# A four-layer image network on one core: three loads change queue, and four durations in the kernel's planning clock change

## The chip, the cores and the metric
The kernel runs on one core of a Trainium2 chip. The metric is the device time of one execution in microseconds (us), where less is better. A core has TensorE (PE, with its weight loads shown as PEld), VectorE (DVE), ScalarE (ACT), GpSimd (POOL) and SyncE (SP). Each executes its own instructions in program order, and they meet at semaphores. ScalarE, SyncE and GpSimd also issue DMAs.

## The reference
Four images of 96 channels and 64 x 64 pixels (L = 4096 positions) go through four residual layers:

```
x = x + scan_layer(groupnorm(x))        # layer 0: a selective scan in four directions
x = x + deformable_conv(groupnorm(x))   # layer 1: 3 x 3 taps at learned positions
t = x as 4096 tokens of 96 channels
t = t + fourier(layernorm(t));  t = t + ffn8(layernorm(t))    # layer 2
t = t + attention(layernorm(t)); t = t + ffn8(layernorm(t))   # layer 3
```

The scan is the large part. For each image b, direction k (4), channel d (192) and state n (16), position after position:

```
h[d,n] = exp(delta[d] * A[d,n]) * h[d,n] + delta[d] * u[d] * B[n]
y[d]   = sum over n of h[d,n] * C[n]
```

B and C depend on the position and on n, delta and u on the position and on d. `ffn8` rounds the inputs and weights of its two products to an 8-bit float format.

## The kernel before, in words
The scan is cut into 4 images x 4 directions x 4 steps of 1024 positions x 3 groups of 64 channels x 8 units: 1536 units, each a tile of 128 partitions (16 states x 8 channels) by 1024 positions. For each unit:

- `fetch` (L874, ScalarE's queue) loads delta into `da`, repeated over the states, five units ahead. Six buffers.
- `decay` (L895, ScalarE) turns `da` into exp(delta A), two units ahead.
- `inflow` (L901, PE) spreads delta u over the states with two products of 96 x 128 by 96 x 512. The three bfloat16 parts of delta u, which together stand for a float32 value, are summed in the product. The result `db` is in one of two PSUM buffers, one unit ahead.
- `recur` (DVE) multiplies `db` by B (L915), then runs the scan instruction (L918) into `hh`.
- `weigh` (POOL) keeps the last column as the next state (L925) and multiplies `hh` by C (L927).
- `total` (PE, L946) sums over the states of two units into `py`; after eight units `settle` (ACT, L957) copies `py` into `yb` and `store` (SyncE, L964) writes it out.

`fetch_step` loads B and C (`bc`, two issues at L881) once for each step of 1024 positions, that is for 24 units. It does so at n mod 24 = 12, twelve units ahead of their first use. `fetch_block` loads the delta u parts (`du0` and `du1`, two issues at L889) once for eight units. It does so at n mod 8 = 2; `inflow` first needs them at n mod 8 = 7. Both have two buffers.

Around the scan there are two streams of side work, written as Python generators that give out a few instructions and then a `cost`. The stream `ends` does, for every image, the preparation of its scan (convolution, projections, `steps`) and later layers 2 and 3 (`Layers23.image`, which starts by loading `t`). The stream `middle` does the close of layer 0 (`behind`) and layer 1 (`Layer1.image`: offsets, then 288 indirect gathers at L1249, their weighting at L1258, transposes at L1272, the product at L1286 and the result `xo`, stored at L1293). Layers 2 and 3 of an image need its layer 1, which needs its whole scan.

The order of all instructions is fixed when the program is built, by a simulated clock (`Clock`). It keeps a planned end for each of PE, DVE, ACT and POOL. After each unit of the scan, its `unit` adds the least unit time PACE to a due time:

```
def now(self):
    return max(self.ends[DVE], self.due) if self.own is None else self.own
def unit(self, scanned):
    self.due += PACE
```

Then the streams may put in steps as long as `has_room` says that no engine a step uses is planned further ahead of now than `AHEAD` (3 us for PE and DVE, 5 for ACT, 7 for POOL), and that DVE's side work in this unit is under 6 us. Each scan stage adds its own planned time: `inflow` 1.1 on PE, `recur` 1.22 and 2.33 on DVE, `weigh` 2.55 on POOL, `total` 1.5 on PE for two units, and 1.3 more for the first two of eight. A `fetch` of `da` adds 0.6 on ACT; the loads of `bc` and `du` add nothing. So a planned duration decides where instructions stand, not how long they take. When the scan is over, the streams go on alone with five PSUM banks for `ends`.

Of the kernel before, what the change touches and what calls it, by code (L numbers as in the profile page):

```python
# [21 lines left out]
DI, NS, R, KG = 192, 16, 6, 4  # L22
D2 = DI - 128
T = 1024
# [7 lines left out]
D8 = 8  # L32
# [149 lines left out]
def cost(pe=0.0, dve=0.0, act=0.0, pool=0.0, **more):  # L182
    return Step((pe, dve, act, pool), **more)


def wait(us=0.0, **more):

    return Step((0.0,) * 4, us, **more)
# [5 lines left out]
PE, DVE, ACT, POOL = range(4)  # L194
# [2 lines left out]

BESIDE = 6.0

PACE = 4.9  # L200


class Clock:
# [306 lines left out]
class Layer0:  # L510
# [365 lines left out]
    def fetch_step(self, u):  # L876

        u.bc = self.sp.tile([128, 2, T], F32, name=f"bc{u.key}", tag="bc")
        for s in range(2):
            src = self.bc_d[u.b][u.k][NS * s : NS * s + NS, u.ts]  # L880
            self.net.nc.scalar.dma_start(u.bc[:, s, :], src.unsqueeze(1).to_broadcast([NS, D8, T]))  # L881

    def fetch_block(self, u):

        u.du = []
        for q in range(2):
            t = self.sp.tile([96, T], BF16, name=f"du{u.key}_{q}", tag=f"du{q}")
            c0 = 64 * u.g + 32 * q
            self.net.nc.scalar.dma_start(t, self.du_d[u.b][u.k][:, c0 : c0 + 32, u.ts])  # L889
            u.du.append(t)  # L890

    def decay(self, u):
# [2 lines left out]
        self.net.nc.scalar.activation(u.da, u.da, AF.Exp, scale=self.al[:, a : a + 1])  # L895

    def inflow(self, u):
        u.spread = self.net.clock.add(PE, 1.1, self.scanned[1])
        db = self.ps.tile([128, 2, CH], F32, name=f"db{u.key}", tag="db", bufs=2)
        for h in range(2):  # L900
            self.net.nc.tensor.matmul(  # L901
                db[:, h, :],
                lhsT=self.rep[:96, u.s % 4, :],
                rhs=u.du[u.s // 4][:, h * CH : (h + 1) * CH],
                start=True,
                stop=True,
            )
        u.db = db.rearrange("p h t -> p (h t)")
# [162 lines left out]
class Layer1:  # L1071
# [41 lines left out]
    def offsets(self, b, om):  # L1113

        net = self.net
        tc, nc = net.tc, net.nc
        with tc.tile_pool(name=f"l1a{b}", bufs=1, side="right") as pre:
            x = pre.tile([C, L], F32, name=f"x1_{b}", tag="x")
            nc.sync.dma_start(x, self.x1[b])
            wom = net.load("wom", pre)  # L1120
            pad = pre.tile([C, PW, PW], F32, name=f"pad1_{b}", tag="pad")
            for edge in (pad[:, 0, :], pad[:, PW - 1, :], pad[:, :, 0], pad[:, :, PW - 1]):
                nc.gpsimd.memset(edge, 0.0)
            yield wait(4.0)
            stats = []
            yield from net.group_norm_stats(x, pre, f"1_{b}", stats)
            mean, rstd = stats
            nmr = pre.tile([C, 1], F32, name=f"nmr{b}", tag="nmr")
            nc.vector.scalar_tensor_tensor(nmr, mean, -1.0, rstd, ALU.mult, ALU.mult)
            yield cost(dve=0.2)  # L1130
            def filled(j):
                cs = slice(j * CH, (j + 1) * CH)
                nc.scalar.activation(x[:, cs], x[:, cs], AF.Identity, scale=rstd, bias=nmr)
                yield cost(act=0.8)
                nc.gpsimd.tensor_copy(
                    pad[:, 1 + j * NR : 1 + (j + 1) * NR, 1 : 1 + W],
                    x[:, cs].rearrange("p (h w) -> p h w", w=W),
                )
                yield cost(pool=0.7)

            yield from pipe(self.net, (filled(j) for j in range(NCH)), 2)
            v = self.views[b % 2]

            def chunk(j):
                r0 = j * NR
                po = net.mm(f"po{b}_{j}", 96)
                for k in range(9):
                    dy, dx = divmod(k, 3)
                    nc.tensor.matmul(  # L1149
                        po,  # L1150
                        lhsT=wom[:, k, :],
                        rhs=pad[:, r0 + dy : r0 + dy + NR, dx : dx + W],
                        start=(k == 0),
                        stop=(k == 8),
                    )
                    if k in (2, 5):
                        yield cost(pe=2.6, holds=1, takes="oc" if k == 5 else "")
                oc = pre.tile([27, CH], F32, name=f"oc{b}_{j}", tag="oc")
                nc.scalar.activation(oc, po[:27], AF.Identity, bias=net.vec(V_OMB, 27))
                yield cost(pe=2.6, act=0.7, new=True, takes="pix")  # L1160

                pt = net.mm(f"pt{b}_{j}")[:, : 4 * C].rearrange("p (q c) -> p q c", c=C)
                for q in range(4):
                    t = 4 * j + q
                    nc.tensor.transpose(pt[:, q, :], x[:, 128 * t : 128 * t + 128], net.ident[:C, :C])
                pix = pre.tile([128, 4, C], F32, name=f"pix{b}_{j}", tag="pix", bufs=2)
                nc.scalar.copy(pix, pt)
                pm = net.mm(f"pm{b}_{j}")[:, : 4 * 27].rearrange("p (q c) -> p q c", c=27)
                for q in range(4):
                    nc.tensor.transpose(pm[:, q, :], oc[:, 128 * q : 128 * q + 128], net.ident[:27, :27])  # L1170
                nc.scalar.copy(om[:, 4 * j : 4 * j + 4, :], pm)
                yield cost(pe=1.6, act=0.8, frees="oc")
                for q in range(4):
                    dy, dx = divmod(q, 2)
                    for r in range(2):
                        y0 = 2 + r0 + r - dy
                        dst = v[y0 : y0 + 7 : 2, 2 - dx : 2 - dx + W, q * C : (q + 1) * C]
                        nc.sync.dma_start(dst.rearrange("t w d -> w t d"), pix[64 * r : 64 * r + 64])
                yield wait(frees="pix")

            yield from pipe(self.net, (chunk(j) for j in range(NCH)), 3, oc=1, pix=2)
# [291 lines left out]
class Ffn:  # L1473
# [23 lines left out]
    def run(self, b, t):  # L1497
        net, n = self.net, self.n
        tc, nc = net.tc, net.nc
        with tc.tile_pool(name=f"fb{n}_{b}", bufs=1) as big, tc.tile_pool(name=f"fs{n}_{b}", bufs=2) as pool:  # L1500
# [3 lines left out]
            def chunk(j):  # L1504
                yield wait(takes="xq")
                cs = slice(j * CH, (j + 1) * CH)
                key = f"f{n}_{b}_{j}"
                xq = pool.tile([C, CH], F8, name=f"xq{key}", tag="xq")
                nc.gpsimd.tensor_copy(xq, tl[:, cs], saturate=False)  # L1509
                yield cost(pool=0.8, new=True, takes="h16")  # L1510
                h16 = pool.tile([128, 3, CH], F16, name=f"h16{key}", tag="h16")
                for g in range(3):
                    ph = net.mm(f"ph{key}_{g}")
                    nc.tensor.matmul(ph, lhsT=self.w1[:, 128 * g : 128 * g + 128], rhs=xq, start=True, stop=True)
                    nc.scalar.copy(h16[:, g], ph)
                yield cost(pe=2.2, act=1.8, frees="xq")
                if net.own_banks:
                    for g in range(3):
                        bias = self.bias[:, g : g + 1]
                        nc.vector.tensor_scalar(h16[:, g], h16[:, g], bias, 0.0, ALU.add, ALU.max)  # L1520
                    yield cost(dve=1.5, takes="h8")
                else:
                    for g in range(3):
                        nc.scalar.activation(h16[:, g], h16[:, g], AF.Relu, bias=self.bias[:, g : g + 1])
                    yield cost(act=2.1, takes="h8")
                h8 = pool.tile([128, 3, CH], F8, name=f"h8{key}", tag="h8")
                nc.gpsimd.tensor_copy(h8, h16, saturate=False)
                yield cost(pool=1.5, new=True, takes="o16", frees="h16")
                po = net.mm(f"po{key}")
                for g in range(3):  # L1530
                    nc.tensor.matmul(po, lhsT=self.w2[:, g, :], rhs=h8[:, g], start=(g == 0), stop=(g == 2))
                o16 = pool.tile([C, CH], F16, name=f"o16{key}", tag="o16")
                nc.scalar.copy(o16, po[:C])
                if net.own_banks:
                    yield cost(pe=2.1, act=0.6, frees="h8")
                    nc.vector.tensor_scalar_add(o16, o16, self.bias[:C, 3:4])
                else:
                    nc.scalar.activation(o16, o16, AF.Identity, bias=self.bias[:C, 3:4])
                    yield cost(pe=2.1, act=1.3, frees="h8")
                nc.vector.tensor_add(t[:, cs], t[:, cs], o16)  # L1540
                yield cost(dve=1.0, frees="o16")

# [174 lines left out]
```

## Time and profile before

| | |
|---|---|
| median of 3 runs | 9321.19 us (9300.55 to 9330.13) |
| profiled execution | 9297.4 us span, mean granted TensorE clock 0.815 |
| busy share of the span | PE 75%, PEld 34%, DVE 73%, ACT 45%, POOL 69% |
| scan, first to last unit | about 371 to 8018 us |
| DMA | 1609.10 MB; ScalarE's queue (q10) 985.79 MB, SyncE's (q1) 390.76, GpSimd's (q0) 226.57 |
| loads that the change touches | 128 issues of `bc` of 512 KB, 384 of `du` of 192 KB |

Busy shares are averages over stages that have different limits. A row of a group gives line, engine, operation and tiles, then the count, the busy time, the mean of one, and the idle time of its engine just before it with what ended that. A wait is read as "who, at which line, waited for whom: us in total, times, longest". Matmul ends are modelled, so a busy PE is not PE at its peak.

### The profile page before, as it was taken

The numbers are of one execution on the slowest core, as the hardware profiler recorded it, in microseconds if no ns is written. First come the engines' busy times: TensorE is split into PE (matmuls) and PEld (weight loads), VectorE is DVE, ScalarE is ACT, GpSimd is POOL, SyncE is SP. The second block draws the span as 40 slices with busy tenths as digits, with TensorE's granted clock in tenths as the row PEclk, the third lists the DMA queues.
The fourth block names the chain that finished last, engine by engine and source line by source line (L and its number), as shares of the span: only waits on it lengthen the run. The fifth ranks groups of instructions, "written<-read, shape, count | busy, mean of one in ns | idle before, by whom it ended". The sixth has DMA issues, their size and how long they took to land.

```text
span 9297.4 us, 93700 instructions
## 1 busy us (share of the span) xinstructions
PE 6961.3 (75%) x32696; PEld 3186.5 (34%) x32696; DVE 6749.8 (73%) x4484; ACT 4200.7 (45%) x5798; POOL 6459.2 (69%) x4755
## 2 busy tenths in 40 slices
PE   6665967696766768777766887777887776887787
PEld 2111311131222233212223553222555321566574
DVE  0378878787888888778887889888888898523313
ACT  4574667465544434566542334553323355312223
POOL 0486678666789998688899976765989677347501
PEclk8676977797877788878788888877888888888898
DMA  1466777677877887787877877767878766544220
GB/s 49 128 192 177 194 201 210 174 195 180 214 201 198 210 204 190 188 207 213 215 208 195 210 189 200 175 166 182 210 197 208 176 176 175 122 123 128 65 64 12
DMA packets 775821, 1609.10 MB, mean 173 GB/s; under 512 B 247665, under 2 KB 338829, under 8 KB 773238
## 3 DMA queue, kind: packets, MB, share of 16 engines
q10 hardware_dynamic: 300672, 985.79, 42.0%
q1 hardware_dynamic: 400950, 390.76, 15.3%
q0 software_dynamic: 73728, 226.57, 9.0%
q8 instruction: 260, 4.26, 0.2%
q14 instruction: 211, 1.73, 0.1%
HBM read 1346.50 MB, written 256.29 MB: 172 GB/s over the span
## 4 chain that ended last, share of the span: by engine, by line
PE 28%; POOL 27%; DVE 17%; DMA 12%; issue 9%; ACT 6%; SPq 1%; ACTq 1%; DVEq 0%; another core or an unknown queue 0%; POOLq 0%
POOL hh L927 12%; POOL g L1249 9%; DVE hh L918 8%; PE pc L662 4%; DVE db L915 4%; PE py L946 3%; PE ps L1272 2%; PE f L1363 2%; PE db L901 2%; POOL lw L750 2%; POOL st L925 1%; DMA da<-de 1%; POOL w L749 1%; PE pd L1286 1%; PE po L1149 1%
## 5 line engine op out<-in xcount | busy, mean ns | idle before, releaser
L927 POOL TENSOR_TENSOR hh<-hh,bc 128x1024 f32<-128x1024 f32 x1536 | 3654.6, 2381 | 388.0 <-DVE hh L918 281.9
L918 DVE TENSOR_TENSOR_SCAN hh<-da,st,db 128x1024 f32<-128x1024 f32 x1152 | 2703.6, 2347 | 240.2 <-PE py L946 77.3
L895 ACT ACTIVATE da<-da,w_al 128x1024 f32<-128x1024 f32 x1536 | 1740.0, 1147 | 1178.0 <-DMA da<-de 504.7
L915 DVE TENSOR_TENSOR db<-db,bc 128x1024 f32<-128x1024 f32 x1536 | 1868.0, 1216 | 498.5 <-PE db L901 447.7
L1249 POOL DMA_INDIRECT g<-table,idx x1152 | 1409.8, 1224 | 438.7 <-issue 239.6
L901 PE MATMUL db<-du,rep 96*128 96x512 bf16 x3072 | 1091.9, 444 | 736.2 <-DVE hh L918 679.8
L946 PE MATMUL py<-hh,w_fold 128*32 128x512 f32 x6144 | 1168.4, 748 | 224.4 <-POOL hh L927 189.0
L918 DVE TENSOR_TENSOR_SCAN hh<-da,db 128x1024 f32<-128x1024 f32 x384 | 878.2, 2287 | 82.3 <-ACT da L895 19.2
L1272 PE MATMUL ps<-w_ident,g 128*96 128x128 f32 x4608 | 716.8, 320 | 287.1 <-issue 116.3
L901 PEld LDWEIGHTS <-rep 96*128 96x128 bf16 x3072 | 277.3, 105 | 1734.5 <-issue 1174.3
L1258 DVE TENSOR_TENSOR g<-g,wt 128x3456 f32<-128x3456 f32 x128 | 555.8, 4343 | 376.8 <-DMA g<-table,idx 360.4
L1272 PEld LDWEIGHTS ps<-w_ident,g 128*96 128x96 f32 x4608 | 624.4, 150 | 477.7 <-issue 200.8
L925 POOL COPY st<-hh 128x1 f32<-128x1 f32 x1152 | 300.3, 261 | 637.3 <-DVE hh L918 591.8
L1280 ACT COPY st<-ps 96x384 f32<-96x384 f32 x384 | 181.9, 476 | 1016.3 <-PE ps L1272 750.5
L749 POOL TENSOR_TENSOR w<-w,ex 128x512 f32<-128x512 f32 x192 | 247.9, 1291 | 491.0 <-ACT w L746 490.4
L662 PE MATMUL pc<-pad,wc 96*128 96x512 f32 x1152 | 536.5, 613 | 51.4 <-DMA wc<-wc_d 46.4
L752 DVE SCALAR_TENSOR_TENSOR rl<-pd,lw 128x512 f32<-128x512 f32 x192 | 131.3, 684 | 494.4 <-POOL lw L750 467.0
L946 PEld LDWEIGHTS py<-hh,w_fold 128*32 128x32 f32 x6144 | 169.7, 121 | 804.6 <-issue 399.2
L771 PE MATMUL pr<-ex,w_ident 128*128 128x512 f32 x384 | 291.5, 850 | 184.9 <-POOL ex L755 79.0
L1509 POOL CAST xqf<-fl 96x512 fp8e5<-96x512 f32 x64 | 44.5, 703 | 507.3 <-DVE fl L1467 457.3
L662 PEld LDWEIGHTS pc<-pad,wc 96*128 96x128 f32 x1152 | 220.7, 196 | 340.2 <-issue 317.9
L1372 ACT COPY d<-f 128x512 f32<-128x512 f32 x192 | 112.4, 585 | 446.5 <-PE f L1363 336.6
(247 smaller groups left out, 9579.0 us busy)
## 6 DMA issues: line engine op xcount, KB each, us to landing
da<-de ACTq DMA_DIRECT2D x1536, 512.0 KB
du<-du ACTq DMA_DIRECT2D x384, 192.0 KB
bc<-bcd ACTq DMA_DIRECT2D x128, 512.0 KB
du<-du SPq DMA_DIRECT2D x128, 384.0 KB
y<-yb SPq DMA_DIRECT2D x384, 128.0 KB
de<-rl SPq DMA_DIRECT2D x128, 256.0 KB
m<-in_dft SPq DMA_DIRECT2D x128, 256.0 KB
du<-du SPq DMA_DIRECT2D x128, 192.0 KB
```

The source lines that it names most:

```text
L662: nc.tensor.matmul(pp, lhsT=wc[:, q, g * 128 : (g + 1) * 128], rhs=pad[:, r0 + dy : r0 + dy + NR, dx : dx + W], start=(q == 0), stop=(q == 8),
L749: nc.gpsimd.tensor_sub(w1, w1, ex)
L895: self.net.nc.scalar.activation(u.da, u.da, AF.Exp, scale=self.al[:, a : a + 1])
L901: self.net.nc.tensor.matmul(db[:, h, :], lhsT=self.rep[:96, u.s % 4, :], rhs=u.du[u.s // 4][:, h * CH : (h + 1) * CH], start=True, stop=True,)
L915: nc.vector.tensor_mul(u.db, u.db, u.bc[:, 0, :])
L918: nc.vector.tensor_tensor_scan(u.along(u.hh), u.along(u.da), u.along(u.db), first, ALU.mult, ALU.add)
L925: self.net.nc.gpsimd.tensor_copy(u.state[:, u.n : u.n + 1], u.hh[:, last : last + 1])
L927: self.net.nc.gpsimd.tensor_mul(u.hh, u.hh, u.bc[:, 1, :])
L946: nc.tensor.matmul(py[p0 : p0 + 32], lhsT=self.fold[:, u.i, :], rhs=hc[:, h * CH : (h + 1) * CH], start=u.sums["add"] is None and u.i == 0 ...
L1249: nc.gpsimd.indirect_dma_start(out=g[:, k, :], out_offset=None, in_=self.tables[b % 2], in_offset=bass.IndirectOffsetOnAxis(ap=idx[:, 9 * ...
L1258: nc.vector.tensor_mul(g4, g4, w4.unsqueeze(2).to_broadcast([128, 36, C]))
L1272: nc.tensor.matmul(pt[:, k, :], lhsT=g[:, k0 + k, c * C : (c + 1) * C], rhs=net.ident, is_transpose=True, start=(c == 0), stop=(c == 3),)
```

## The change
The loads of B and C (L881) and of delta u's parts (L889) are issued on SyncE's queue in place of ScalarE's, at the same places in the program's text. In the clock, PACE goes from 4.9 to 4.8 us, and planned PE durations go down: of the spreading products from 1.1 to 0.8, of the transposes of a chunk of pixels from 1.6 to 1.2, of the first 8-bit product of a chunk from 2.2 to 1.3 and of the second from 2.1 to 1.3. What is computed stays the same.

```
-PACE = 4.9
+PACE = 4.8
...
     def fetch_step(self, u):
...
-            self.net.nc.scalar.dma_start(u.bc[:, s, :], src.unsqueeze(1).to_broadcast([NS, D8, T]))
+            self.net.nc.sync.dma_start(u.bc[:, s, :], src.unsqueeze(1).to_broadcast([NS, D8, T]))
...
     def fetch_block(self, u):
...
-            self.net.nc.scalar.dma_start(t, self.du_d[u.b][u.k][:, c0 : c0 + 32, u.ts])
+            self.net.nc.sync.dma_start(t, self.du_d[u.b][u.k][:, c0 : c0 + 32, u.ts])
...
     def inflow(self, u):
-        u.spread = self.net.clock.add(PE, 1.1, self.scanned[1])
+        u.spread = self.net.clock.add(PE, 0.8, self.scanned[1])
...
-                yield cost(pe=1.6, act=0.8, frees="oc")
+                yield cost(pe=1.2, act=0.8, frees="oc")
...
-                yield cost(pe=2.2, act=1.8, frees="xq")
+                yield cost(pe=1.3, act=1.8, frees="xq")
...
-                    yield cost(pe=2.1, act=0.6, frees="h8")
+                    yield cost(pe=1.3, act=0.6, frees="h8")
...
-                    yield cost(pe=2.1, act=1.3, frees="h8")
+                    yield cost(pe=1.3, act=1.3, frees="h8")
```

## Prediction
> **What bounds the kernel now.** I read the page's chain first, to see whether one engine carries the end, then busy time by stage, then who makes VectorE (DVE) wait during the scan, then what the two DMA-issuing queues wait for, then the durations of what the change touches.
>
> The chain of waits, shares by engine:
> ```profile
> PE 28%; POOL 27%; DVE 17%; DMA 12%; issue 9%; ACT 6%; SPq 1%; ACTq 1%; DVEq 0%; another core or an unknown queue 0%; POOLq 0%
> ```
> No engine owns the path: PE and POOL share half, and ScalarE with its queue has 7%. The stretches, cut where the scan begins and ends and where the last image starts its final layers:
> ```profile
> core 0: us, PE busy (x) PEld busy (x) DVE busy (x) ACT busy (x) POOL busy (x), PEclk, DMA share, GB/s
> 371.00:8018.00 7647.00, 5692.40 (x25058) 2343.22 (x25058) 6343.43 (x4002) 3705.45 (x4936) 5953.75 (x4342) 0.81 0.75 194
> 8018.00:8870.00 852.00, 684.39 (x4190) 495.89 (x4186) 251.38 (x245) 203.69 (x408) 426.15 (x343) 0.84 0.36 102
> 8870.00:9297.00 427.00, 356.51 (x2999) 258.98 (x2998) 129.12 (x185) 130.61 (x256) 40.15 (x33) 0.92 0.11 34
> ```
> The scan holds 7647 of 9297 us, with DVE busy 83%, POOL 78%, PE 74%. Its 1536 units take 4.98 us each, against a least unit time of 4.9 in the kernel's clock. Then comes a tail of 1279 us in which PE is busiest (80% and 83%): the rest of image 2's last layers beside image 3's sampling, then image 3 alone. The rows by tile show the load of `t` at 4925, 6266, 7824 and 8845 us: images 0 and 1 took 1341 and 1558 us beside the scan, while image 3 took 445 us alone. Image 2 had run 194 us when the scan ended. Side work not done inside the scan is thus paid for in the tail.
>
> DVE's waits inside the scan (engine, line, awaited: us, times, longest):
> ```profile
> DVE db L915 <- PE db L901: 431.1, 204, 26.8
> DVE rl L752 <- POOL lw L750: 192.2, 99, 9.7
> DVE g L1258 <- DMA g<-table,idx: 127.9, 40, 7.8
> DVE hh L918 <- PE py L946: 89.3, 77, 6.1
> DVE hh L918 <- ACT da L895: 31.8, 10, 11.8
> ```
> Of 7647 - 6343 = 1304 us of idle DVE, a third waits for the spreading product (L901), which stands in PE's queue behind side work. ScalarE is last only for 32 us.
>
> SyncE's queue in the same stretch:
> ```profile
> SPq L964 <- ACT yb L957: 1053.6, 105, 33.7
> SPq L964 <- DMA da<-de: 854.8, 70, 29.6
> SPq L1293 <- DVE xo L1291: 613.2, 41, 31.5
> ```
> SyncE does little, but it stands at stores for up to 34 us. The second line tells something else: a store waits for the landing of a load that ScalarE issued. Issues of both queues are coupled by their completion semaphores.
>
> The durations (min/median/max ns):
> ```profile
> L901 PE MATMUL db<-du,rep x3072: 376/379/634, 363.5 to 8009.5; 96*128 96x512 bf16 x192
> L889 ACTq DMA_DIRECT2D du<-du x384: 718/734/1293, 352.8 to 7957.2; - x192
> L881 ACTq DMA_DIRECT2D bc<-bcd x128: 522/610/1642, 351.5 to 7852.0; - x128
> L1514 PE MATMUL phf<-xqf,w1q x192: 376/389/634, 5801.9 to 9280.2; 96*128 96x512 fp8e5 x192
> ```
>
> **What the Trainium skill says.** "DMA: Bandwidth & Descriptors", section "Issuing engines are not separate DMA queues": DMAs run on the same 16 engines whoever starts them, and another issuer saves only the sequencer's time. The trace agrees that the engines are shared (75% busy in the scan), and gives that time: 0.61 and 0.73 us each. "TensorE: Matmul & The Clock Gate", "Weight-path perf modes": 8-bit products without DoubleRow run at the 16-bit rate. The trace agrees: least duration 376 ns in both rows. Its "Architectural detail" section says that ScalarE and VectorE are strictly first in, first out; ScalarE's waits for `du` landings ahead of `da` (80.6 us in the waits) fit that.
>
> **The change part by part.** No arithmetic is added or removed. Three things alter.
>
> *Queue.* 128 issues of B and C and 384 of delta u leave ScalarE: 128 x 0.61 + 384 x 0.734 = 360 us. SyncE gets them. It has 2037 issues and waits most of the time, so its own time is free. On ScalarE the activations `da` and later `da` loads move forward, but only 7% of the chain passes there and 32 us of DVE waits end there: I take 10 us of gain, between 0 and 40 (the 32 us and a little through PE). Bytes stay the same (128 x 512 KB, 384 x 192 KB), so the transfer engines gain nothing. On SyncE these loads queue behind stores and `xo` stores, and whoever needs them is `inflow` on PE, then DVE. delta u is asked for at n mod 8 = 2 and first used by `inflow` at n mod 8 = 7: 5 units, 25 us. B and C have 12 units, 60 us. The waits are mostly SyncE arriving early, their mean being 1053.6 / 105 = 10 us. So the cost I take is 0; its upper bound is a rival below. The lower bound is nothing, as an earlier landing serves nobody: no PE wait for `du` above 20 us in total is listed.
>
> *PE durations.* These are numbers in the clock that orders the program: lower ones admit more side work per unit. Before, a unit of 4.9 leaves 4.9 - 1.1 (spreading) - 0.91 (1.5 for two folds plus an eighth of 1.3) = 2.89 us of PE for side work; after, 4.8 - 0.8 - 0.91 = 3.09. Over 1536 units: 4439 to 4746, +307. The 8-bit chunks of images 0 and 1 inside the scan, 32, give 32 x (0.9 + 0.8) = 54, and the pixel step 24 x 0.4 = 10. Together 371 us, 8.4% more. Is PE what limits the side streams in that clock? PE is the first engine of nearly every side step, but gathers are limited by POOL and normalizations by DVE. I take two thirds: 247 us. The other third loses with the shorter unit: a third of 0.1 x 1536 = 154, or 51. Net 196 us of side time, which is 196 / 1450 (mean of images 0 and 1) = 13.5% of an image; in the tail that is 0.135 x 445 = 60 us. Bounds: 0 and all 371, 26% or 114 us. It costs DVE inside the scan 0.135 x 129 = 17 us.
>
> The new values are nearer the trace for spreading (two products, 0.76 us at the median), yet optimistic for 8 bits (mean rows 3 x 0.496 = 1.49 against 1.3). More side work ahead of L901 makes DVE wait longer: growing with the room, 0.084 x 431 = 36 us. Bounds: a fifth less (-86), half more (+215).
>
> *Least unit time.* DVE's own work, 1868.0 + 2703.6 + 878.2 = 5450 us, does not shrink. What can shrink is the rest of the scan, 7647 - 5450 = 2197 us, thinned by 0.1 / 4.9: 45 us. Bounds: 0 (engines set each unit) and 154 (the clock sets all).
>
> Sum: -10 - 60 - 45 + 17 + 36 = -62 us. The profiled span is 9297.4, giving 9235; that execution lies at the low end of the runs (9300.55 to 9330.13, median 9321.19), so the forecast of the median is 9321 - 62 = 9259.
>
> **The rivals.**
> *Order gains fully:* all 371 us are used, tail -114; with 40 us from ScalarE and the same other terms: -40 - 114 - 45 + 33 + 36 = -130, or 9191. For it: PE heads the chain. Against: POOL follows within 1%.
>
> *Nothing measurable:* the numbers permute the order, DVE and POOL set the pace, and the thinner scan is repaid in the tail: about 9310. For it: of sixteen equal groups of units in the timeline, eight have a median spacing of 3.6 to 3.7 us, which is DVE's own 1.22 + 2.35, under either least unit time. This includes the case that the change doesn't do what it says: the loads moved, but nobody waited for them.
>
> *Slower, by PE:* side work now admitted ahead of L901 makes DVE the one that waits. Place: L915 waiting for L901. Price: at 40% growth 172 us, -98 + 172 = +74, or 9395. It decides from 98 / 431 = 23% growth. For it: the waits are already DVE's largest. Against: real products take less than planned, and two `db` buffers are filled ahead.
>
> *Slower, by SyncE:* a wait of 33.7 us exceeds the 25 us of lead by 8.8; in 15 of 192 blocks that is 132 us: +70, or 9391. The coupled semaphores could pass such a delay on to `da` loads. Against: the mean wait is 10 us.
>
> **How the numbers follow.** Forecast 0.50 (its own range 9215 to 9300), full gain 0.15, nothing 0.14, slower by PE 0.15, by SyncE 0.06. About 0.3% (28 us) is what a measurement of this kernel can tell from no change. Faster by more: 0.46 of the forecast and 0.15, 0.61. Within: 0.04 and 0.14, 0.18. Slower: 0.21. The range takes 9160 (full gain with a little more from the unit time) to 9385, leaving out the worst of the slower cases.
>
> **What would show it.** Right: the scan ends 20 to 60 us earlier, with image 2 further along (its `t` load earlier than 7824), the stretch up to image 3's load shorter than 827 us, ScalarE's queue at 843 MB and SyncE's at 533 (985.79 and 390.76 less and plus 143), and L915 waiting 400 to 500 us for L901. Wrong: L915's wait above 530 us, PE idle on `du` landings, or the scan ending later than 8018 with an unchanged tail.

## The result and the profile after

The changed kernel took 9245.26 us (median of 4 runs, 9238.72 to 9250.81), the kernel before 9310.87 in the same comparison. The ratio is 0.9931, with a 95% interval of 0.9903 to 0.9959: faster by 0.7%, about 64 us. The forecast was a gain of 62 us. The profiled spans are 9297.4 and 9238.5 us, 59 us apart.

First the stretches of the changed kernel, cut as before at the scan's end and at image 3's load of `t` (columns as in the table shown for before):
```profile
366.00:8024.00 7658.00, 5697.58 (x25940) 2383.80 (x25939) 6368.45 (x4017) 3709.60 (x4972) 5950.06 (x4341) 0.81 0.75 194
8024.00:8785.00 761.00, 575.97 (x3280) 420.56 (x3276) 231.54 (x232) 174.61 (x353) 427.97 (x343) 0.83 0.38 105
8785.00:9238.00 453.00, 374.65 (x3028) 265.94 (x3028) 128.93 (x185) 138.63 (x270) 39.14 (x33) 0.90 0.12 36
```
The scan ends at 8025 us, where it ended at 8016 before. Its end did not come earlier, though it now holds more of the late layers. In this pair of profiles the whole gain is in the stretch up to image 3's load. From the timelines, load starts of `t` for images 2 and 3 and the last gather of image 3's sampling. Before:
```profile
7824.26 0.33 SPq L1621 DMA_DIRECT2D t<-x  x1
...
8729.65 0.95 POOL L1249 DMA_INDIRECT g<-table,idx  x1 [0.30 <-issue]
...
8844.55 0.30 SPq L1621 DMA_DIRECT2D t<-x  x1
```
After:
```profile
7618.74 0.34 SPq L1621 DMA_DIRECT2D t<-x  x1
...
8739.58 0.96 POOL L1249 DMA_INDIRECT g<-table,idx  x1 [0.16 <-issue]
...
8785.15 0.30 SPq L1621 DMA_DIRECT2D t<-x  x1
```
The span is a sum of four pieces: the scan's end; from there to the start of the last gather of image 3's layer 1 (713 us before, 715 after); from that gather to image 3's load of `t`, which waits until image 2 is through its own late layers (115 us before, 46 after); and image 3 alone (453 in both). Image 2 started 205 us earlier, and image 3 waits 69 us less for it.

VectorE's waits after the change, in the stretch that the prediction uses for before (371 to 8018 us):
```profile
DVE db L915 <- PE db L901: 406.7, 195, 24.8
DVE rl L752 <- POOL lw L750: 214.4, 97, 14.4
DVE g L1258 <- DMA g<-table,idx: 103.9, 32, 8.8
DVE hh L918 <- PE py L946: 88.6, 70, 9.7
...
DVE hh L918 <- ACT da L895: 29.3, 12, 6.7
```
The wait for the spreading product is 24 us shorter than before (431.1). The queues moved the bytes that were forecast:
```profile
q10 hardware_dynamic: 244224, 843.17, 35.9%
q1 hardware_dynamic: 457398, 533.38, 21.4%
```
And few wait for the loads that now stand on SyncE. The instruction's row, and who waited for it (us, times):
```profile
L889 SPq DMA_DIRECT2D du<-du x384: 4/747/11757, 346.8 to 7942.6; - x192
...
  PE db L901: 31.2, 6
  ACT da L895: 27.1, 5
  PEld L901: 25.8, 5
```
PE waited for delta u six times in 1536 units, and 26 of these 31 us lie at the first two units, where before it also waited 18 us. The chain of waits of the changed kernel is followed back only a little way (its shares sum to 13%), so it is not compared.

### The profile page after: what moved, and what is told of

Same layout as the page of the kernel before. It is cut to its first block, busy times and chain, and to the rows that moved or that the text cites. A ratio compares the mean times of both kernels' runs of the same rounds, so it can differ in the third digit from the quotient of the medians.

```text
span 9238.5 us, 94079 instructions
## 1 busy us (share of the span) xinstructions
PE 6872.1 (74%) x32696; PEld 3157.4 (34%) x32696; DVE 6754.7 (73%) x4484; ACT 4186.6 (45%) x5798; POOL 6456.4 (70%) x4755
## 2 busy tenths in 40 slices
DMA packets 775825, 1609.14 MB, mean 174 GB/s; under 512 B 247665, under 2 KB 338829, under 8 KB 773238
## 5 line engine op out<-in xcount | busy, mean ns | idle before, releaser
L915 DVE TENSOR_TENSOR db<-db,bc 128x1024 f32<-128x1024 f32 x1536 | 1867.2, 1216 | 466.0 <-PE db L901 428.0
L901 PE MATMUL db<-du,rep 96*128 96x512 bf16 x3072 | 1083.5, 441 | 811.5 <-DVE hh L918 750.3
L1272 PE MATMUL ps<-w_ident,g 128*96 128x128 f32 x4608 | 696.1, 314 | 256.8 <-DVE g L1258 121.6
L901 PEld LDWEIGHTS <-rep 96*128 96x128 bf16 x3072 | 275.4, 105 | 1781.1 <-issue 1196.6
L739 PE MATMUL pd<-xd,w_dtw 103*64 103x512 f32 (+1 forms) x512 | 261.2, 779 | 67.6 <-DVE rl L752 27.4
```

Source lines behind the costliest of these rows:

```text
L901: self.net.nc.tensor.matmul(db[:, h, :], lhsT=self.rep[:96, u.s % 4, :], rhs=u.du[u.s // 4][:, h * CH : (h + 1) * CH], start=True, stop=True,)
L915: nc.vector.tensor_mul(u.db, u.db, u.bc[:, 0, :])
L1272: nc.tensor.matmul(pt[:, k, :], lhsT=g[:, k0 + k, c * C : (c + 1) * C], rhs=net.ident, is_transpose=True, start=(c == 0), stop=(c == 3),)
```

## The experiments

Each is the kernel before, or the changed kernel, with the edit shown. Ratios are to the kernel before on the same chip, with their 95% intervals. The events of the profiled executions are collected here and used below, in us. "Lead" is by how much image 2's load of `t` precedes the scan's end (negative where it comes after), "wait" the time from image 3's last gather to its load of `t`, and "steps" the start of the last of image 3's `steps` products at L739, with how many of their 128 were done when image 1's gathers began. One profile stands for each kernel, and its time can differ from the median of all runs: that of durations_only is 18 us above, that of no_queue 12 us below. The runs also come from several chips, on which the kernel before had medians of 9284 to 9314 us. So differences of scan ends are good to some 20 or 30 us; the ratios are firmer.

| run | ratio | scan end | lead | wait | span | steps |
|---|---|---|---|---|---|---|
| before | 1 | 8016 | 192 | 115 | 9297 | 4864 (96) |
| queue_only | 0.9979 | 7998 | 199 | 113 | 9279 | 4843 (96) |
| durations_only | 1.0017 | 8161 | 519 | 19 | 9338 | 4599 (126) |
| spread_only | 1.0014 | 8126 | 482 | 19 | 9305 | 4595 (128) |
| pace_only | 1.0099 | 7913 | -225 | 316 | 9407 | 5049 (78) |
| the change | 0.9931 | 8025 | 406 | 46 | 9239 | 4665 (112) |
| no_pace | 0.9906 | 8049 | 505 | 19 | 9213 | 4548 (126) |
| no_queue | 0.9998 | 8091 | 410 | 45 | 9301 | 4700 (112) |
| after_479 | 1.0058 | 7988 | -11 | 184 | 9374 | 5048 (80) |
| after_470 | 1.0037 | 7884 | -210 | 289 | 9325 | 5129 (64) |
| durations_bc | 0.9985 | 8117 | 510 | 19 | 9294 | 4594 (126) |
| durations_du | 0.9942 | 8065 | 516 | 19 | 9254 | 4536 (126) |
| pace_500 | 1.0067 | 8184 | 658 | 20 | 9341 | 4403 (128) |
| ends_first_479 | 1.0006 | 8075 | 502 | 19 | 9282 | 4311 (128) |

**The parts alone.** The first four runs make one part of the change each. queue_only:
```
-            self.net.nc.scalar.dma_start(u.bc[:, s, :], ...
+            self.net.nc.sync.dma_start(u.bc[:, s, :], ...
-            self.net.nc.scalar.dma_start(t, self.du_d[...
+            self.net.nc.sync.dma_start(t, self.du_d[...
```


> Before, with only the loads of B, C and delta u's parts moved to SyncE's queue; the clock's numbers and so the order of every engine's own work stay those of before. Theory (the gain comes from planned PE durations, which let side work into the scan, so that the tail shrinks by 60 us): ratio 0.997 to 1.001, the scan still ends near 8018 us, image 2's t is loaded near 7824. Rival (ScalarE, relieved of 360 us of issues, is what gained): ratio 0.992 to 0.995, with the scan or the last image's start 50 us earlier. Rival (late loads on SyncE cost time, which the other parts win back): ratio above 1.003 and PE waiting for du at L901.

Measured: 0.9979 (0.9966 to 0.9991), the scan ending 19 us earlier. The ratio is in the theory's range and not in a rival's. The gain, about 20 us, is twice the prediction's 10 and a third of the whole.

durations_only (all five planned durations) and spread_only (the first line alone):
```
-        u.spread = self.net.clock.add(PE, 1.1, self.scanned[1])
+        u.spread = self.net.clock.add(PE, 0.8, self.scanned[1])
...
-                yield cost(pe=1.6, act=0.8, frees="oc")
+                yield cost(pe=1.2, act=0.8, frees="oc")
...
-                yield cost(pe=2.2, act=1.8, frees="xq")
+                yield cost(pe=1.3, act=1.8, frees="xq")
...
-                    yield cost(pe=2.1, act=0.6, frees="h8")
+                    yield cost(pe=1.3, act=0.6, frees="h8")
...
-                    yield cost(pe=2.1, act=1.3, frees="h8")
+                    yield cost(pe=1.3, act=1.3, frees="h8")
```


> Before, with only the planned PE durations lowered (spreading 0.8, pixels 1.2, both 8-bit products 1.3). Theory: most of the gain, ratio 0.990 to 0.996; image 2's t is loaded 150 to 250 us earlier than 7824, the scan ends where it did or up to 50 us later, and the tail is shorter. Rival (the durations only permute the order and the gain is from the queue or the unit time): ratio 0.998 to 1.002.

> Before, with only the spreading product's planned duration lowered from 1.1 to 0.8, which by the clock's numbers is 461 of the 525 us of PE time that the durations free. Theory: nearly all that durations_only gains, ratio 0.991 to 0.997. Rival (the 8-bit durations, which act in the tail too, do it): ratio 0.998 to 1.002 while durations_only is below it by 0.003 or more.

Measured: 1.0017 (1.0010 to 1.0025) and 1.0014 (1.0005 to 1.0024). The theory missed both. The ratio of durations_only is where its rival had it, but not for the rival's reason: image 2's lead grew by 327 and 290 us and the wait for it fell from 115 to 19 us, as the theory had it, but the scan ended 145 and 110 us later, and that took it all back. The two runs agree in time, so the 8-bit and pixel durations add next to nothing to that of spreading.

pace_only:
```
-PACE = 4.9
+PACE = 4.8
```


> Before, with only the least unit time lowered from 4.9 to 4.8. Theory as in the prediction: the scan ends up to 45 us earlier and side work falls back by up to 150 us of its time in the scan, which the tail pays with 45 us: ratio 0.995 to 1.003, image 2's t loaded later relative to the scan's end. Rival (engines set each unit): the scan ends where it did, ratio 0.999 to 1.004. Rival (any change of the order shifts the time by half a per cent either way): a ratio outside 0.995 to 1.004.

Measured: 1.0099 (1.0079 to 1.0118). The scan ended 104 us earlier, more than twice the 45 of the prediction, but image 2 started 314 us later, after the scan's end, and image 3 waited 316 us for it. The ratio is outside the theory's range and where the last rival had it. My theory that the durations bring the gain fell here, for none of the parts alone comes near 0.9931. A new one: the time is the scan's end plus a tail that depends on the lead, and durations and unit time move along this trade in opposite directions.

**One part taken out of the change.** no_pace is the change with `PACE = 4.9`, no_queue the change with both loads on `nc.scalar` again; after_479 and after_470 have these values:
```
-PACE = 4.8
+PACE = 4.79
...
-PACE = 4.8
+PACE = 4.7
```


> The change without its shorter least unit time (4.9 again). New theory (the time is the scan's end plus a tail that loses about 0.31 us for each us by which image 2's load of t leads the scan's end; lower PE durations lengthen both the scan and the lead, a shorter unit time shortens both): the scan ends near 8140, image 2's lead is near 500 us, the tail near 1180; ratio 0.998 to 1.002. Rival (durations and queue help by themselves and the unit time adds nothing): ratio 0.991 to 0.996.

> The change with the loads back on ScalarE's queue: durations and unit time together. New theory: the gain of the change stands but for the queue's 20 us: ratio 0.993 to 0.997, scan end near 8040, lead near 400. Rival (parts add up as measured alone, +0.0017 and +0.0099): ratio 1.008 to 1.014. Rival (the queue matters more when the order is denser): ratio 0.998 to 1.003.

> The change with a least unit time of 4.79 in place of 4.80: a tenth of the step in that number. New theory (smooth trade): within 0.003 of the change's 0.9931, scan end 10 us earlier, lead 10 to 40 us shorter. Rival (any small change of the numbers permutes the order and shifts the time by half a per cent): more than 0.004 away from 0.9931, either way.

> The change with a least unit time of 4.7. New theory: another 100 us off the scan's end, near 7920, and a lead near 200 us with a tail near 1280 if the lead falls by about 200 us, so a span near 9200: ratio 0.986 to 0.992. Rival (the lead falls by some 400 us as when 4.9 became 4.8 alone, and the tail takes back more than the scan gives): ratio 0.995 to 1.005.

Measured: no_pace 0.9906 (0.9888 to 0.9923), faster than before; whether it is also faster than the change is not clear, as its interval overlaps that of 0.9931 (0.9903 to 0.9959); no_queue 0.9998 (0.9987 to 1.0009); after_479 1.0058 (1.0045 to 1.0071); after_470 1.0037 (1.0025 to 1.0049). All four missed the new theory. no_queue, after_479 and after_470 landed where a rival had them (the queue matters more in a denser order; a small change of the numbers permutes the order; the tail takes back more than the scan gives). The theory failed in two ways.

First, the queue. The clock knows nothing of it, so no_queue has the changed kernel's order of work, and durations_only that of no_pace. With the order held, moving the loads took 67 us off the scan's end in one pair, 113 in the other, and 19 in the order of before. It is the largest single gain, and it depends on the order. Durations and unit time alone (no_queue) come to nothing, 0.9998: they shorten the wait by 69 us and end the scan 75 us later. Moving the loads takes 67 of these 75 us back.

Second, a hundredth of a microsecond in the unit time cost 1.3%. The lead fell from 406 to -11 us. Where it was lost shows in the `steps`: in the stream `ends`, those of image 3 stand ahead of the late layers of all images. They end 383 us later than in the change (5048 against 4665), and image 0's load of `t` comes 387 us later. In after_479, the products of L739 of image 3 before and after the start of image 1's gathers (stretch, us, PE busy and count, PEld busy and count, clock, share of DMA, GB/s):
```profile
4007.00:4516.00 509.00, 45.94 (x80) 11.86 (x80) 0.79 0.77 202
4516.00:5049.00 533.00, 22.82 (x48) 6.28 (x48) 0.74 0.78 208
```
One product each 6.4 us before the gathers, one each 11.1 us beside them. In before:
```profile
3919.00:4540.00 621.00, 50.36 (x96) 13.72 (x96) 0.79 0.79 208
4540.00:4865.00 325.00, 13.80 (x32) 4.04 (x32) 0.75 0.81 214
```
6.5 and 10.2 us. So the products that are left when the gathers begin take longer. In the table, 126 to 128 done give an end of `steps` near 4600 or before, 112 give 4665 to 4700, 96 about 4850, 78 to 80 about 5050 and 64 gives 5129. The stream of layer 1 has the first turn in each round, and both want POOL (4.0 planned us for a chain of `steps`, 1.3 for a gather). This count, the phase of the two streams, is not all of it, for half of the 383 us were lost one image earlier. Image 2's steps end at 3382 us in after_479 and at 3196 in the change; they too stand beside gathers, those of image 0, with 56 of their 128 done when these begin in after_479 and 64 in the change. Why a hundredth of a microsecond does this was not followed further back.

**Which load, and is it the phase.** The last four. durations_bc and durations_du each move one of the two loads of queue_only, on top of durations_only. pace_500 is the change with PACE at 5.0. ends_first_479 is after_479 with this:
```
-            return any([stream.step() for stream in reversed(streams)])
+            return any([stream.step() for stream in streams])
```


> durations_only with the loads of B and C alone moved to SyncE's queue (128 issues, 78 us of ScalarE's time); the order of the engines' own work is that of durations_only (1.0017) and no_pace (0.9906). Theory ring (1 MB of B and C ahead of the da loads in one queue makes those land late; of the 113 us between the two scans, units 13 to 16 of 24, right after the load of B and C, hold 75): two thirds of the way to no_pace, ratio 0.992 to 0.996, scan end near 8080. Rival (ScalarE's issue time, of which B and C are 78 of 360 us): a fifth of the way, ratio 0.998 to 1.001.

> durations_only with delta u's parts alone moved (384 issues, 282 us). Theory ring: a third of the way to no_pace, ratio 0.997 to 1.000, scan end near 8120. Rival (issue time, 282 of 360 us): four fifths of the way, ratio 0.991 to 0.995.

> The change with a least unit time of 5.0. Theory of the phase (what decides is how many of the 128 products of image 3's steps stand before image 1's gathers; at 4.9 it is 126 of them, so nothing is left to win there): all 128 before the gathers, scan end 60 to 110 us later than no_pace's 8048, image 2's lead 100 to 300 us longer, tail 30 to 90 us shorter; ratio 0.989 to 0.996. Rival (a longer unit time goes on to gain as from 4.8 to 4.9): ratio below 0.988.

> after_479 (1.0058) with one more change: in each round the stream of preparation and last layers takes its turn before the stream of layer 1, in place of after it. Theory of the phase (after_479 is slow because 48 of image 3's 128 step products were left when image 1's gathers began, and those then take turns behind the gathers): the steps of image 3 end before 4800 instead of 5048, image 2's lead is above 200 us instead of -12; ratio 0.990 to 1.000, unless layer 1 of image 3 in the tail is delayed. Rival (permuted order as such): steps end near 5050 still and ratio 1.003 to 1.009.

Measured: durations_bc 0.9985 (0.9975 to 0.9994), durations_du 0.9942 (0.9925 to 0.9959). From 1.0017 to 0.9906 is 0.0111; B and C make 0.0032 of it, 29%, delta u 0.0075, 68%, and the two add up. The theory that the megabyte of B and C ahead of the `da` loads does it falls, and both ratios are where the rival had them: the shares are near those of the issue time (78 and 282 of 360 us; 22% and 78%). ScalarE's idle time ahead of `decay` and VectorE's ahead of L915 show where the freed time went. Rows of durations_only (count, busy us, mean ns, idle before):
```profile
L895 ACT ACTIVATE da<-da,w_al 128x1024 f32<-128x1024 f32 x1536 | 1745.7, 1148 | 1228.8 <-DMA da<-de 546.5
L915 DVE TENSOR_TENSOR db<-db,bc 128x1024 f32<-128x1024 f32 x1536 | 1869.1, 1217 | 548.7 <-PE db L901 507.4
```
Of no_pace:
```profile
L915 DVE TENSOR_TENSOR db<-db,bc 128x1024 f32<-128x1024 f32 x1536 | 1869.0, 1217 | 491.0 <-PE db L901 464.0
L895 ACT ACTIVATE da<-da,w_al 128x1024 f32<-128x1024 f32 x1536 | 1744.0, 1149 | 899.0 <-DMA da<-de 411.5
```
ScalarE is idle 330 us less ahead of `da`, and VectorE 58 us less ahead of L915, mostly for PE. Time in which a queue issues DMAs counts as idle, but the 330 us are not issue time alone. ScalarE's waits ahead of `da` in the scan of durations_only:
```profile
ACT da L895 <- DMA da<-de: 528.9, 192, 13.1
ACT da L895 <- DMA du<-du: 130.8, 79, 11.4
ACT da L895 <- issue: 114.6, 108, 10.2
```
Of no_pace:
```profile
ACT da L895 <- DMA da<-de: 398.7, 163, 14.5
```
The waits that end with a landing of delta u fell from 131 to 8 us, and those named "issue" from 115 to 39. So a rival stays: ScalarE was also relieved of standing for landings of these loads, and no run separates that from their issue time.

ScalarE reaches VectorE through PE: PE's queue stands at products that wait for ScalarE's copies, and the spreading product stands behind them. Three of these waits of PE in durations_only:
```profile
PE pr L775 <- ACT du L773: 103.0, 66, 6.1
PE pr L772 <- ACT du L768: 65.8, 41, 6.5
PE py L941 <- ACT yb L957: 64.3, 30, 10.3
```
In no_pace:
```profile
PE pr L775 <- ACT du L773: 90.9, 64, 6.5
PE pr L772 <- ACT du L768: 54.6, 35, 4.7
PE py L941 <- ACT yb L957: 53.2, 26, 6.4
```
Summed over all lines in the scan, moving the loads changed PE's idle time that ended with ScalarE, and VectorE's that ended with PE and directly with ScalarE, like this (us):

| order | PE, for ScalarE | VectorE, for PE | VectorE, for ScalarE |
|---|---|---|---|
| of before (before, queue_only) | 309 to 289 | 607 to 597 | 81 to 46 |
| of the change (no_queue, the change) | 353 to 289 | 650 to 576 | 69 to 71 |
| of durations_only (durations_only, no_pace) | 350 to 281 | 695 to 594 | 90 to 75 |

In the two denser orders most of what VectorE gained (74 and 102 us) was time for which it had waited for PE. In the order of before that path gave 10 us.

pace_500: 1.0067 (1.0051 to 1.0084), not 0.989 to 0.996. The lead grew as expected, from no_pace's 505 to 658 us, yet the wait stayed at 20 us while the scan ended 135 us later, not 60 to 110. ends_first_479: 1.0006 (0.9993 to 1.0018), from 1.0058, just past its expected range. `steps` ended at 4311 and the lead came to 502 us, as the theory of the phase had it. But the turn changes the whole order: image 3's steps also began 579 us earlier (3428 against 4007) and image 1's gathers 318 us later. So the run shows that the order of the two streams sets the lead, and not that the count alone does.

Over all fourteen profiles the wait is one falling curve of the lead: 316 at -225, 289 at -210, 184 at -11, about 114 near 195, 45 near 408, and 19 to 20 from 482 on. Between 192 and 406 it falls by 0.32 us for each us. From about 480 on it stays at 19 to 20 us, and more lead buys nothing.

## Why the prediction was right, and where it was not

The size was right: -62 us forecast, which is 0.7%, and the interval of the ratio holds it. That is luck in its make-up. The forecast had 52 us from the order (the terms for PE durations, unit time, scan work and waits: -60 - 45 + 17 + 36) and 10 from the queue. With the loads left on ScalarE the order gave 0.9998 (0.9987 to 1.0009), about 2 us, and moving them in that order about 62. The error in one cancelled that in the other.

- *PE durations and unit time, the tail's 60 us.* The mechanism was right: an earlier image 2 shortens the wait of image 3. The net size was right too: 196 us of side time forecast, 205 measured (load of `t`, 7824 to 7619); 60 us of tail forecast, 69 measured; 0.31 us for each us of lead used, 0.32 measured. no_queue, with the order alone, has the same 69. But the two terms behind the 196, 247 us from the durations less 51 for the unit time, do not fit: alone they moved the lead by +327 and -418. That more lead buys nothing beyond about 480 us was not foreseen.
- *PE durations, the price in the scan.* I took 17 us of work and 36 of waits, 53 together. durations_only ended its scan 145 us later in its profile (its slowest run, 18 us above the median): more than twice that. The wait of L915 for L901 grew from 431 to 491 us over that run's scan, +60 against 36. The rival "slower, by PE" had the right place; in the change itself the other parts took that back (406.7).
- *Queue, "10 us of gain, between 0 and 40".* This step failed. With the order held, the loads were worth 0.9931 against 0.9998, about 62 us, and 0.9906 against 1.0017 without the shorter unit time, about 103. I bounded it by ScalarE's 7% of the chain and the 32 us for which VectorE's scan waits for it directly. That ScalarE's delay reaches VectorE as a wait for PE, under another name, was put at "a little"; in these two orders VectorE waited 74 and 102 us less for PE. The estimate fits only the order of before, where 0.9979 is about 20 us.
- *Least unit time, 45 us of gain.* It shortens the scan, by 104 us alone and by 24 us within the change (8049 to 8025). Alone it costs more than it gives, 1.0099. Within the change, 0.9931 against 0.9906 points the same way, but the intervals overlap; that it helps is not shown. The working counted the lost side time only for the third of the streams that PE does not limit, 51 us, and did not see that a lead can collapse.
- *SyncE.* Right: no late loads that matter, 31 us of PE waits in six cases, 26 of them at the first two units.
- *The sign "the scan ends 20 to 60 us earlier"* was wrong, and against my own sum, whose terms inside the scan give -45 + 17 + 36 - 10 = -2. Measured: +8. From before by way of durations_only and no_pace it is +145 - 113 - 24.

One way through the parts is +16 us for durations, about -103 for the queue in their order, and +23 (not clear of noise) for the unit time. Another is -2 for durations and unit time together and -62 for the queue. The queue in the order of before is worth 20 and the order alone 2, together 64: the change is faster because the denser order and the relieved ScalarE go together.

What stays open: relieving ScalarE is worth about 20, 62 or 103 us by the ratios in three orders (19, 67 and 113 by the scan's end). The pairs show that it is so, that delta u and B and C add up, and that in the denser orders it comes by way of PE; which of ScalarE's other instructions carry it, and how much is issue time and how much standing for landings, was not separated. Lead and phase are read from one profile per kernel.

## What to carry to other kernels

When an order is fixed by a simulated clock, read its effect as two numbers, when the main chain ends and how far the side work has come by then, and find the lead from which more side work no longer shortens the tail. An engine that seldom releases the bottleneck directly can still hold it through a third one, so price its issue time by taking it away with the order held. And treat a small gain from one value of a clock as one point of a rough curve: here 4.79, 4.8 and 4.9 gave 1.0058, 0.9931 and 0.9906.

## What the runs showed of the hardware

One issue of these loads holds its queue about equally long on either engine: at the median 0.734 us on ScalarE and 0.747 on SyncE for delta u, and 0.610 and 0.583 for B and C. The planning clock had this at nothing. The transfers were the same, 1609.10 and 1609.14 MB in all, with the DMA engines 75% busy in the scan before and after. With the order of all other work held, only the issuer changed, and the scan's end moved by 19, 67 and 113 us.
